# Gate and up as two 64-row tiles side by side in a selective-scan and feed-forward kernel

## The chip, the cores and the metric

The kernel runs on one core of a Trainium2 chip. The metric is the device time of one execution in microseconds (us). A core has five engines with instruction queues of their own: TensorE (PE in the profile; its weight loads are shown as PEld), VectorE (DVE), ScalarE (ACT), GpSimd (POOL) and SyncE (SP), which issues most transfers. PSUM, the memory that TensorE writes, has eight banks here, each 128 partitions by 512 floats.

## The reference, cut to what matters

The input is 2 sequences of 1024 tokens with 512 features, all float32. A selective-scan layer and a feed-forward layer follow, each with a residual and a layer norm:

```python
xn = x * rsqrt(mean(x * x) + 1e-6) * norm_w
xn = xn * sigmoid((xn @ select_proj_w.T + b) * gate)
delta, B, C = split(xn @ x_proj_w.T)              # 128 each
delta = softplus(delta @ dt_proj_w.T + dt_b)      # 512
h = exp(delta * A) * h + (delta * xn) * B         # per token: 512 x 128 states
y = sum over states of h * C
x = layernorm(x + (y + x * D) @ out_proj_w.T)
gate, up = x @ w_gate.T, x @ w_up.T               # 512 -> 2048 each
x = layernorm(x + (silu(gate) * up) @ w_down.T)   # 2048 -> 512
```

The recurrence over h is the long part: 512 x 128 states for each of 2048 tokens. The feed-forward layer is the part that the change rewrites: gate and up both contract over the same 512 features of x (called x1 in the kernel) and give 2048 hidden values each.

## The kernel before, in words

**The loop.** The scan is cut into stretches of 32 tokens (st), each into two half-states h of 8 steps; the main loop (from line 819) has 132 half-states, 1056 steps k. The place of a step in its half-state is r = k % 8. One step does 128 x 32 columns of states. On PE it issues first `state_mm` (line 523, writes bu, four matmuls of 64 rows and 256 columns in fp32r, two row halves b = 0, 1 side by side) and then `decay_mm` of the next step (line 510, writes a, four matmuls of the same shape). ACT copies the carried column of h into bu (line 854) and takes the exponential of a (line 529, two instructions). DVE then runs the scan instruction (line 861) over 1024 columns. POOL makes du, the moving operand of bu, two steps ahead (line 487). bu has two buffers, a has two tiles (one step's), so PE can be ahead of DVE by little more than a step.

**What PE does besides.** After these eight matmuls a step has room for other TensorE work.
- y: the products with C (`y_round`, line 538), eight rounds of 16 matmuls per half-state, always of the half-state before; 128 rows, 32 columns wide, four column strips side by side. ROUNDS says at which places r they stand: rounds 0 to 3 at r = 1, rounds 4 to 7 at r = 5. `y_out` copies the result at r = 0 of a later half-state.
- everything else is a set of Python generators, run by the class Work (line 742). A generator yields "P" when its next piece wants a PSUM bank and PE, "H" between two parts of such a piece, and "E" when other engines are to go first. There is one bank for all of them (`misc`, line 200, pool ps_m with one buffer). The generator that has it is the holder; `give_back` (line 760) takes it back at the start of a step when the holder is at "E". `tensor` (line 774) runs one part. PARTS says how many parts a place r earns as credit (3 at most places, 0 where y stands, 2 at r = 7: 17 a half-state); a step runs at most 4 parts.
- the generators are `pre` (projections for later tokens: ss, sel, xp, b, z, uT), `y_add` (one transpose yT per stretch), `post` (the output projection op and the first layer norm), `ffn` (gate and up, then the down projection d) and `silu` (no PE work).
- `busy` (line 801) is a filler whose result nobody reads: one matmul of 64 rows and 256 columns in fp32 into the second half of y's bank. A step with r > 0 that ran fewer parts than PARTS[r] gets one.

**Gate and up (line 664 on).** A tile of 128 tokens has NF/2 = 8 groups f. x1 is transposed by four PE transposes into x1T, four blocks of 128 features on 128 partitions (line 656), and copied by ACT (line 660). A group is 32 matmuls of 128 rows, 128 columns and 128 moving columns (line 672): for each of two blocks b of 128 hidden values gate and up, each over four blocks k of features. All four results lie in one bank; two matmuls are one part, so a group is 8 parts. ACT copies the bank to gu with one instruction of 512 columns (line 682), then `silu` runs on POOL and ACT.

**Order.** Nothing is reordered after this program: each engine runs its instructions in the order in which the loop emits them (the schedule is manual). When the loop ends, the generators that are left run out with six banks (from line 884); this is called the tail below.

**PSUM.** y has one bank (its first half holds y, the second the fillers), the generators one, bu four, a two: all eight.

Of the kernel before, what the change touches and what calls it, by code (L numbers as in the profile page):

```python
# [9 lines left out]
FP = mybir.dt.float32  # L10
# [6 lines left out]
P = 128  # L17
# [2 lines left out]

ROUNDS = ((), (0, 1, 2, 3), (), (), (), (4, 5, 6, 7), (), ())
PARTS = (3, 0, 3, 3, 3, 0, 3, 2)
RMS_EPS = 1e-6
LN_EPS = 1e-5

# [9 lines left out]
def kernel(  # L37
# [16 lines left out]
    nc = tc.nc  # L54
# [3 lines left out]
    B, L, D = out.shape  # L58
# [474 lines left out]
    def y_round(h, b):  # L533

        st, i = divmod(h, 2)
        at = 28 + 28 * b
        for q in range(NM):
            nc.tensor.matmul(  # L538
                ys[ts(q, 32), 0, :],
                cz[st % 2][:, at : at + 32],  # L540
                hs[i][q // 2][:, ts(q % 2, 64), ts(b, 4)],
                start=(b == 0), stop=(b == 7), skip_group_check=True,
            )

    def y_out(h):

# [7 lines left out]
            return  # L554
        work.add(y_add(st, yc), front=True)

    zs = {}

    def touched(st):

# [16 lines left out]
    def y_add(st, yc):  # L577

        yield "E"
        yield "E"  # L580
        yr = post_pool.tile([P, P], FP, tag="yr", name=f"yr_{st}")
        nc.gpsimd.tensor_tensor(yc, yc, pick.unsqueeze(1).to_broadcast([P, P, 4]), ALU.mult)  # L582
        yield "E"
        nc.gpsimd.tensor_tensor(yc[:, :, 0:2], yc[:, :, 0:2], yc[:, :, 2:4], ALU.add)
        nc.gpsimd.tensor_tensor(yr, yc[:, :, 0], yc[:, :, 1], ALU.add)
        yield "E"
        yield "E"
        yield "P"
        ps = misc(f"yT_{st}", 1)
        nc.tensor.transpose(ps[:, 0:P], yr, ident)  # L590
        yield "E"
        ps = ps[:, 0:P].rearrange("p (m t) -> p m t", t=S)
        for tt, lo, hi in touched(st):
            z = zs[tt][:, :, lo - tt * P : hi - tt * P]
            nc.vector.tensor_tensor(  # L595
                z, z, ps[:, :, lo - token(st) : hi - token(st)], ALU.add
            )
            if hi == (tt + 1) * P:
                work.add(post(tt), front=True)

    def post(tt):

# [30 lines left out]
    def ffn(tt, row):  # L633
# [15 lines left out]
        while finished[-1] < tt:  # L649
            yield "E"  # L650
        fetch(4)
        x1T = ffn_pool.tile([P, NM, P], FP, tag="x1T", name=f"x1T_{tt}")
        yield "P"
        ps = misc(f"x1T_{tt}", 2)
        for m in range(NM):
            nc.tensor.transpose(ps[:, ts(m, P)], row[:, ts(m, P)], ident)  # L656
            if m == 1:
                yield "H"
        yield "E"
        nc.scalar.copy(x1T, ps.rearrange("p (m t) -> p m t", t=P))  # L660
        hid = ffn_pool.tile([P, NF, P], FP, tag="hid", name=f"hid_{tt}")
        ready, at = [], 0

        for f in range(0, NF, 2):
            fetch(at + 4)
            yield "P"
            ps = misc(f"gu_{tt}_{f}", 2 * NM)
            for b in range(2):
                w = pieces[at + b].rearrange("p (a k h) -> p a k h", a=2, k=NM)
                for a in range(2):  # L670
                    for k in range(NM):
                        nc.tensor.matmul(  # L672
                            ps[:, ts(2 * a + b, P)], w[:, a, k, :], x1T[:, k, :],
                            start=(k == 0), stop=(k == NM - 1),
                        )
                        if k % 2:
                            if a and k + 1 == NM and not b:
                                fetch(at + 5)
                            yield "E" if a and b and k + 1 == NM else "H"
            at += 2  # L680
            gu = ffn_pool.tile([P, 2, 2 * P], FP, tag="gu", name=f"gu_{tt}_{f}", bufs=2)
            nc.scalar.copy(gu, ps.rearrange("p (a t) -> p a t", a=2))  # L682
            work.add(silu(gu, hid[:, f : f + 2, :], f"{tt}_{f}", ready), front=True)
        while len(ready) < NF // 2:
            yield "E"
# [21 lines left out]
    def silu(gu, dst, name, ready):  # L707


        yield "E"  # L710
        e = ffn_pool.tile([P, 2 * P], FP, tag="e", name=f"e_{name}", bufs=2)
        g = gu[:, 0, :]
# [12 lines left out]
        ready.append(dst)  # L725
# [16 lines left out]
    class Work:  # L742


        def __init__(self):

            self.gens, self.holder, self.left = [], None, 0

        def add(self, gen, front=False, late=False):
            item = [gen, next(gen), late]  # L750
# [23 lines left out]
        def tensor(self):  # L774

            if self.holder is not None:
                if self.holder[1] != "H":
                    return False
                self.left -= 1
                self.step(self.holder)  # L780
                return True
            for item in sorted(self.gens, key=lambda item: item[2]):
                if item[1] == "P":
# [14 lines left out]
        for _ in gen:  # L798
            pass

    def busy(start=False):

        nc.tensor.matmul(  # L803
            ys[:, 1, :], ident[0:64, :], sel_w[0:64, 0, 0:256],
            start=start, stop=True, skip_group_check=True,
        )

    run(pre(0))
    state_diag(1)
    busy(True)  # L810
# [8 lines left out]
    for k in range(NG):  # L819
# [1 line left out]
        st, i = divmod(h, 2)  # L821
        r = k % 8

        if PARTS[r]:
            work.give_back()
        if r == 0:
            c = lot_of[st]
            for d in range(c + 1, 3 if c == 0 else c + 2):
# [48 lines left out]
        credit -= done  # L877
    y_out(2 * NS - 2)
    for b in range(8):
        y_round(2 * NS - 1, b)  # L880
    y_out(2 * NS - 1)
    ps_a.release()
    ps_bu.release()
    bank_pool[0] = tc.alloc_tile_pool(name="ps_m2", bufs=6, space=PSUM)
    for pool in (half_pool, step_pool, pre_pool):
        pool.release()
# [8 lines left out]
def _laid_out(i):  # L895
# [65 lines left out]
```

## Time and profile before

| what | value |
|---|---|
| median of three runs | 2681.81 us (2676.76 to 2682.79) |
| profiled execution, its own time | 2689.41 us |
| span of the profiled execution | 2687.6 us |
| first scan to the end of the last scan | 57.4 to 2618.4 us |
| busy: PE, DVE, ACT, POOL | 2488.7, 2424.6, 1767.1, 1708.3 us |
| mean granted TensorE clock | 0.953 |

The profile is of one execution. Its busy times are sums over an engine's instructions; matmuls are pipelined, so a PE busy 93% says only that some matmul was nearly always in flight. A record is one instruction as the profiler saw it: a float32 matmul leaves two weight loads and two matmul records (two passes), an fp32r matmul one of each. The granted clock is the share of full speed that TensorE was given; it is 1.0 or 0.5 at any moment.

### The profile page before, as it was taken

The numbers are of one execution on the slowest core, as the hardware profiler recorded it, in microseconds if no ns is written. First come the engines' busy times: TensorE is split into PE (matmuls) and PEld (weight loads), VectorE is DVE, ScalarE is ACT, GpSimd is POOL, SyncE is SP. The second block draws the span as 40 slices with busy tenths as digits, with TensorE's granted clock in tenths as the row PEclk, the third lists the DMA queues.
The fourth block names the chain that finished last, engine by engine and source line by source line (L and its number), as shares of the span: only waits on it lengthen the run. The fifth ranks groups of instructions, "written<-read, shape, count | busy, mean of one in ns | idle before, by whom it ended". The sixth has DMA issues, their size and how long they took to land.

```text
span 2687.6 us, 61618 instructions
## 1 busy us (share of the span) xinstructions
PE 2488.7 (93%) x23742; PEld 1824.6 (68%) x23742; DVE 2424.6 (90%) x1283; ACT 1767.1 (66%) x4248; POOL 1708.3 (64%) x1923
## 2 busy tenths in 40 slices
PE   4888999999999999999999989999999999999998
PEld 3555666767667676776767667676776767676677
DVE  4999989999899999999999999999999999999990
ACT  3666666767677576776767667676667767566663
POOL 3656575766567575676757657577666857565553
PEclk6998899999999999999999989999999999999999
DMA  3122442344434452444423434235433444243335
GB/s 126 26 57 60 146 129 68 109 153 130 112 95 130 135 144 71 129 115 152 146 78 113 125 102 140 77 118 153 135 110 105 139 136 132 59 144 88 114 108 196
DMA packets 329009, 309.49 MB, mean 115 GB/s; under 512 B 184896, under 2 KB 257856, under 8 KB 328592
## 3 DMA queue, kind: packets, MB, share of 16 engines
q1 hardware_dynamic: 326656, 303.16, 38.1%
q8 instruction: 192, 3.15, 0.5%
q0 software_dynamic: 800, 1.97, 0.2%
q14 instruction: 97, 0.79, 0.1%
q10 hardware_dynamic: 1264, 0.43, 0.1%
HBM read 263.46 MB, written 41.94 MB: 114 GB/s over the span
## 4 chain that ended last, share of the span: by engine, by line
PE 37%; DVE 14%; ACT 2%; issue 1%; POOL 0%; POOLq 0%; DVEq 0%; ACTq 0%
DVE h L861 13%; PE gu L672 11%; PE y L538 8%; PE bu L523 6%; PE a L510 4%; PE d L693 3%; PE y L803 1%; PE sel L247 1%; ACT a_sb L529 1%; PE op L611 0%; PE xp L247 0%; ACT bu L854 0%; PE x1T L656 0%; DVE stats_a L731 0%; DVE x L699 0%
## 5 line engine op out<-in xcount | busy, mean ns | idle before, releaser
L861 DVE TENSOR_TENSOR_SCAN h<-a_sb,bu 128x1024 f32<-128x1024 f32 x1056 | 2353.1, 2273 | 168.3 <-ACT bu L854 155.2
L487 POOL TENSOR_TENSOR du<-u_r,hot 128x512 fp32r<-128x512 f32 x1056 | 1112.1, 1058 | 598.6 <-PE bu L523 528.0
L529 ACT ACTIVATE a_sb<-a 128x496 f32<-128x496 f32 x2112 | 1122.9, 585 | 83.0 <-PE a L510 71.7
L523 PE MATMUL bu<-du,b_r 64*128 64x256 f32 x4224 | 623.1, 341 | 89.6 <-DVE h L861 73.7
L854 ACT COPY bu<-h 128x32 f32<-128x32 f32 x1024 | 224.3, 219 | 685.4 <-PE bu L523 609.8
L523 PEld LDWEIGHTS bu<-du,b_r 64*128 64x128 f32 x4224 | 396.5, 190 | 358.7 <-issue 156.1
L538 PE MATMUL y<-h,cz 128*32 128x256 f32 x8448 | 556.6, 407 | 0.1
L672 PE MATMUL gu<-x1T,w 128*128 128x128 f32 x4096 | 542.9, 284 | 9.2 <-DVE zT L595 4.8
L510 PE MATMUL a<-ddt,a_r 64*128 64x256 f32 x4224 | 515.7, 295 | 23.9 <-DVE c_sb L305 9.0
L672 PEld LDWEIGHTS gu<-x1T,w 128*128 128x128 f32 x4096 | 485.2, 193 | 55.1 <-ACT gu L682 10.7
L510 PEld LDWEIGHTS a<-ddt,a_r 64*128 64x128 f32 x4224 | 385.8, 191 | 43.5 <-ACT a_sb L529 21.5
L538 PEld LDWEIGHTS y<-h,cz 128*32 128x32 f32 x8448 | 260.0, 115 | 201.0 <-issue 44.3
L693 PE MATMUL d<-w,hid 128*128 128x256 f32 x1024 | 265.5, 400 | 5.2 <-DVE zT L595 3.7
L693 PEld LDWEIGHTS d<-w,hid 128*128 128x128 f32 x1024 | 185.5, 193 | 46.4 <-DVE zT L595 4.6
L803 PE MATMUL y<-sel_w,ident 64*128 64x256 f32 x572 | 195.8, 423 | 0.0
L713 POOL TENSOR_SCALAR gu<-gu 128x256 f32<-128x256 f32 x128 | 108.1, 845 | 125.7 <-ACT gu L682 125.5
L722 POOL TENSOR_TENSOR hid<-gu,e 128x256 f32<-128x256 f32 x128 | 93.5, 730 | 40.4 <-ACT e L719 38.7
L682 ACT COPY gu<-gu 128x512 f32<-128x512 f32 x128 | 75.1, 587 | 61.8 <-PE gu L672 60.3
L803 PEld LDWEIGHTS y<-sel_w,ident 64*128 64x128 f32 x572 | 88.4, 192 | 34.5 <-issue 21.4
L714 POOL TENSOR_TENSOR gu<-gu 128x256 f32<-128x256 f32 x128 | 93.4, 729 | 10.7
L582 POOL TENSOR_TENSOR yc<-yc,pick 128x512 f32<-128x512 f32 x66 | 68.7, 1041 | 32.8 <-ACT yc L552 32.8
L247 PE MATMUL sel<-xT,sel_w 128*128 128x256 f32 (+1 forms) x288 | 69.5, 381 | 10.0 <-ACT dt L289 6.0
(120 smaller groups left out, 1217.4 us busy)
## 6 DMA issues: line engine op xcount, KB each, us to landing
w<-in_wgu_s_dram SPq DMA_DIRECT2D x256, 512.0 KB, 3.9
w<-in_wd_s_dram SPq DMA_DIRECT2D x128, 512.0 KB, 3.8
u_r<-u_d SPq DMA_DIRECT2D x262, 64.0 KB, 3.1
ddt<-dt_d SPq DMA_DIRECT2D x934, 16.0 KB, 2.2
b_r<-b_d SPq DMA_DIRECT2D x130, 64.0 KB, 3.2
u_d<-uTh SPq DMA_DIRECT2D x15, 512.0 KB, 3.7
u_d<-uT SPq DMA_DIRECT2D x15, 512.0 KB, 4.7
dt_d<-xT SPq DMA_DIRECT2D x56, 128.0 KB, 2.1
```

The source lines that it names most:

```text
L247: nc.tensor.matmul(ps[:, 0:n], w[:, k, ts(m, P)], rhs[:, k, :], start=(k == 0), stop=(k == NM - 1),)
L487: nc.gpsimd.tensor_tensor(dus[k], us[h][:, :, ts(4 * mm + 2 * pair + s, 16)].unsqueeze(3).to_broadcast([P, 2, 16, 16]), hot16.unsqueeze(1) ...
L510: nc.tensor.matmul(ps[:, ts(e, 8), :], a_r[rows, pair, 4 * (2 * i + mm) + x, :], ddts[i][rows, :, 2 * x + mm, :], start=(e == 0), stop=(e ...
L523: nc.tensor.matmul(bu[:, ts(b, 16), ts(j, 16)], prepared[k // 16][rows, j, :], du[rows, j, :, :], start=(j == 0), stop=(j == 1), skip_grou ...
L529: nc.scalar.activation(a_sb[:, k % 3, ts(b, 16), 1:], ps[:, :, 1:], AF.Exp, scale=-1.0)
L538: nc.tensor.matmul(ys[ts(q, 32), 0, :], cz[st % 2][:, at : at + 32], hs[i][q // 2][:, ts(q % 2, 64), ts(b, 4)], start=(b == 0), stop=(b == ...
L672: nc.tensor.matmul(ps[:, ts(2 * a + b, P)], w[:, a, k, :], x1T[:, k, :], start=(k == 0), stop=(k == NM - 1),)
L693: nc.tensor.matmul(ps[:, 0:HD], hid[:, f, :], w[:, f % 4, :], start=(f == 0), stop=(f == NF - 1),)
L713: nc.gpsimd.tensor_scalar_max(g, g, -80.0)
L803: nc.tensor.matmul(ys[:, 1, :], ident[0:64, :], sel_w[0:64, 0, 0:256], start=start, stop=True, skip_group_check=True,)
L854: nc.scalar.copy(bu[:, :, 0], states[:, :, S - 1])
L861: nc.vector.tensor_tensor_scan(states.rearrange("p q t -> p (q t)"), a_sb[:, k % 3, :, :].rearrange("p q t -> p (q t)"), bu.rearrange("p q ...
```

## The change

- The weights of gate and up are laid out anew on the host: in each piece partitions 0 to 63 hold gate, 64 to 127 up, in eight blocks k of 64 features (up's blocks are turned by one).
- x1T gets eight blocks: block j holds features 64j to 64j+63 on the lower partitions and the next 64 on the upper. So each half of the partitions has all 512 features. This takes seven transposes and two small matmuls, in two pieces with a bank, two parts and an ACT copy each.
- A group f is now 64 matmuls of 64 rows: for each b and k one for gate on the lower 64 rows and one for up on the upper 64, in turn. Gate's results go to the generators' bank, up's to the second half of y's bank. Four matmuls (two k) are one part; a group is again 8 parts.
- ACT copies up and then gate, 256 columns each, in place of one copy of 512.
- y and up share a bank, and a `start` flag clears flags of the bank. `begin_y` and `begin_up` therefore keep account of who starts first; a group of gate and up asks for PE with "Q", which is granted while y's rounds are not under way, or once in between when y has started the bank.
- ROUNDS puts y's runs at r = 1 and r = 3; PARTS is 3 at the six other places (18 a half-state). `give_back` runs at every place.
- Fillers: where a place with PARTS ran fewer than two parts and no generator holds the bank, `busy` issues one or two pairs of 64-row matmuls, the lower into the generators' bank and the upper into y's (the lower alone while y's rounds are under way).
- `y_add` waits until the stretch before it is summed; silu's exponential is written over gate; in the tail up takes a bank of its own from the six.

```diff
-ROUNDS = ((), (0, 1, 2, 3), (), (), (), (4, 5, 6, 7), (), ())
-PARTS = (3, 0, 3, 3, 3, 0, 3, 2)
+ROUNDS = ((), (0, 1, 2, 3), (), (4, 5, 6, 7), (), (), (), ())
+PARTS = (3, 0, 3, 0, 3, 3, 3, 3)
...
+        if b == 0:
+            work.begin_y()
+        first = b == 0 and work.y_first
...
-        x1T = ffn_pool.tile([P, NM, P], FP, tag="x1T", name=f"x1T_{tt}")
...
+        x1T = ffn_pool.tile([P, 2 * NM, P], FP, tag="x1T", name=f"x1T_{tt}")
+        for m in range(0, 2 * NM, 4):
+            yield "P"
+            ps = misc(f"x1T_{tt}_{m}", 2)
+            for k in range(4):
+                at = 64 * (m + k)
+                if at + P <= D:
+                    nc.tensor.transpose(ps[:, ts(k, P)], row[:, at : at + P], ident)
+                else:
+                    nc.tensor.matmul(ps[0:64, ts(k, P)], row[:, at:], ident, start=True, stop=True)
+                    nc.tensor.matmul(ps[64:P, ts(k, P)], row[:, 0:64], ident, start=True, stop=True)
+                if k == 1:
+                    yield "H"
+            yield "E"
+            nc.scalar.copy(x1T[:, m : m + 4], ps.rearrange("p (m t) -> p m t", t=P))
...
-            yield "P"
-            ps = misc(f"gu_{tt}_{f}", 2 * NM)
+            yield "Q"
+            lo = misc(f"gu_{tt}_{f}", 2 * NM)
+            hi, first = work.begin_up(f"up_{tt}_{f}")
             for b in range(2):
-                w = pieces[at + b].rearrange("p (a k h) -> p a k h", a=2, k=NM)
-                for a in range(2):
-                    for k in range(NM):
+                w = pieces[at + b].rearrange("p (k h) -> p k h", h=P)
+                for k in range(2 * NM):
+                    for a, ps in enumerate((lo, hi)):
                         nc.tensor.matmul(
-                            ps[:, ts(2 * a + b, P)], w[:, a, k, :], x1T[:, k, :],
-                            start=(k == 0), stop=(k == NM - 1),
+                            ps[:, ts(b, P)], w[ts(a, 64), k, :], x1T[ts(a, 64), k, :],
+                            start=(k == 0 and (a == 0 or first and b == 0)), stop=(k == 2 * NM - 1),
+                            skip_group_check=True,
                         )
...
-            nc.scalar.copy(gu, ps.rearrange("p (a t) -> p a t", a=2))
+            nc.scalar.copy(gu[:, 1, :], hi[:, 0 : 2 * P])
+            nc.scalar.copy(gu[:, 0, :], lo[:, 0 : 2 * P])
...
+        def begin_y(self):
+
+            if self.up_open and not self.up_first:
+                while self.up_open:
+                    self.tensor()
+                    self.give_back()
+            self.y_first = not self.up_open
+            self.y_open, self.up_clear = True, self.y_first
+
+        def up_ready(self):
+            return self.tail or not self.y_open or self.up_clear
+
+        def begin_up(self, name):
+
+            self.up_open, self.up_first = True, self.tail or not self.y_open
+            self.up_clear = False
+            if self.tail:
+                return bank_pool[0].tile([P, 512], FP, tag="m", name=name), True
+            return ys[:, 1, :], self.up_first
...
-    def busy(start=False):
+    def busy(name, count):
 
-        nc.tensor.matmul(
-            ys[:, 1, :], ident[0:64, :], sel_w[0:64, 0, 0:256],
-            start=start, stop=True, skip_group_check=True,
-        )
+        if work.holder is not None:
+            return
+        lo = misc(name, 0)
+        for _ in range(count):
+            for a in range(1 if work.y_open else 2):
+                nc.tensor.matmul(
+                    (lo[:, 0:256], ys[:, 1, :])[a], ident[ts(a, 64), :],
+                    sel_w[ts(a, 64), 0, 0:256], start=(a == 0), stop=True, skip_group_check=True,
+                )
...
-        if r and done < PARTS[r]:
-            busy()
+        if PARTS[r] and done < 2:
+            busy(f"fill_{k}", 2 - done)
...
-    gu = gu.reshape(2, -1, P, d // P, P).transpose(1, 4, 0, 3, 2).reshape(-1, P, 2 * d)
+    gu = gu.reshape(2, -1, P, d // 64, 64).transpose(1, 0, 4, 3, 2)
+    gu = np.stack([gu[:, 0], np.roll(gu[:, 1], -1, axis=2)], axis=1).reshape(-1, P, 2 * d)
```

More of the change, by code (lines that the diff above doesn't have):

```diff
@@ L541, in y_round @@
                 hs[i][q // 2][:, ts(q % 2, 64), ts(b, 4)],
-                start=(b == 0), stop=(b == 7), skip_group_check=True,
+                start=first, stop=(b == 7), skip_group_check=True,
             )
+        if b == 7:
+            work.y_open = False
     def y_out(h):
@@ L555, in y_out @@
         work.add(y_add(st, yc), front=True)
-    zs = {}
+    zs, summed = {}, []
     def touched(st):
@@ L587, in y_add @@
         yield "E"
+        while len(summed) < st:
+            yield "E"
         yield "P"
@@ L599, in y_add @@
                 work.add(post(tt), front=True)
+        summed.append(st)
     def post(tt):
@@ L651, in ffn @@
         fetch(4)
-        x1T = ffn_pool.tile([P, NM, P], FP, tag="x1T", name=f"x1T_{tt}")
-        yield "P"
[L654 to L660, printed above, removed]
+        x1T = ffn_pool.tile([P, 2 * NM, P], FP, tag="x1T", name=f"x1T_{tt}")
[11 more added lines that the diff above has]
+                    yield "H"
+            yield "E"
+            nc.scalar.copy(x1T[:, m : m + 4], ps.rearrange("p (m t) -> p m t", t=P))
         hid = ffn_pool.tile([P, NF, P], FP, tag="hid", name=f"hid_{tt}")
@@ L665, in ffn @@
             fetch(at + 4)
-            yield "P"
-            ps = misc(f"gu_{tt}_{f}", 2 * NM)
+            yield "Q"
+            lo = misc(f"gu_{tt}_{f}", 2 * NM)
+            hi, first = work.begin_up(f"up_{tt}_{f}")
             for b in range(2):
-                w = pieces[at + b].rearrange("p (a k h) -> p a k h", a=2, k=NM)
-                for a in range(2):
-                    for k in range(NM):
+                w = pieces[at + b].rearrange("p (k h) -> p k h", h=P)
+                for k in range(2 * NM):
+                    for a, ps in enumerate((lo, hi)):
                         nc.tensor.matmul(
-                            ps[:, ts(2 * a + b, P)], w[:, a, k, :], x1T[:, k, :],
-                            start=(k == 0), stop=(k == NM - 1),
-                        )
[L676 to L679, printed above, removed]
+                            ps[:, ts(b, P)], w[ts(a, 64), k, :], x1T[ts(a, 64), k, :],
+                            start=(k == 0 and (a == 0 or first and b == 0)), stop=(k == 2 * NM - 1),
+                            skip_group_check=True,
+                        )
+                    if k % 2:
+                        if k + 1 == 2 * NM and not b:
+                            fetch(at + 5)
+                        yield "E" if b and k + 1 == 2 * NM else "H"
             at += 2
+            work.up_open = False
             gu = ffn_pool.tile([P, 2, 2 * P], FP, tag="gu", name=f"gu_{tt}_{f}", bufs=2)
-            nc.scalar.copy(gu, ps.rearrange("p (a t) -> p a t", a=2))
+            nc.scalar.copy(gu[:, 1, :], hi[:, 0 : 2 * P])
+            nc.scalar.copy(gu[:, 0, :], lo[:, 0 : 2 * P])
             work.add(silu(gu, hid[:, f : f + 2, :], f"{tt}_{f}", ready), front=True)
@@ L710, in silu @@
         yield "E"
-        e = ffn_pool.tile([P, 2 * P], FP, tag="e", name=f"e_{name}", bufs=2)
-        g = gu[:, 0, :]
+        g = e = gu[:, 0, :]
         nc.gpsimd.tensor_scalar_max(g, g, -80.0)
@@ L747, in __init__ @@
             self.gens, self.holder, self.left = [], None, 0
+            self.y_open = self.y_first = self.up_open = self.up_clear = self.tail = False
+        def begin_y(self):
[13 more added lines that the diff above has]
+            return ys[:, 1, :], self.up_first
         def add(self, gen, front=False, late=False):
@@ L782, in tensor @@
             for item in sorted(self.gens, key=lambda item: item[2]):
-                if item[1] == "P":
+                if item[1] == "P" or item[1] == "Q" and self.up_ready():
                     self.holder = item
@@ L799, in run @@
             pass
-    def busy(start=False):
-        nc.tensor.matmul(
-            ys[:, 1, :], ident[0:64, :], sel_w[0:64, 0, 0:256],
-            start=start, stop=True, skip_group_check=True,
-        )
+    def busy(name, count):
[8 more added lines that the diff above has]
+                )
     run(pre(0))
     state_diag(1)
-    busy(True)
+    nc.tensor.matmul(ys[:, 1, :], ident, sel_w[:, 0, 0:256], start=True, stop=True)
     bank_pool.pop().release()
@@ L822 @@
         r = k % 8
-        if PARTS[r]:
-            work.give_back()
+        work.give_back()
         if r == 0:
@@ L874 @@
             done += 1
-        if r and done < PARTS[r]:
-            busy()
+        if PARTS[r] and done < 2:
+            busy(f"fill_{k}", 2 - done)
         credit -= done
+    while work.up_open:
+        work.tensor()
+        work.give_back()
     y_out(2 * NS - 2)
@@ L883 @@
     ps_bu.release()
+    work.tail = True
     bank_pool[0] = tc.alloc_tile_pool(name="ps_m2", bufs=6, space=PSUM)
```

## The prediction

> **What bounds the kernel now.** I read the busy rows first: PE 93%, DVE 90%, so two engines share the limit and neither is enough by itself. Then the group rows, for the scan, gate and up, and the filler:
>
> ```profile
> PE 2488.7 (93%) x23742; PEld 1824.6 (68%) x23742; DVE 2424.6 (90%) x1283; ACT 1767.1 (66%) x4248; POOL 1708.3 (64%) x1923
> ...
> L861 DVE TENSOR_TENSOR_SCAN h<-a_sb,bu 128x1024 f32<-128x1024 f32 x1056 | 2353.1, 2273 | 168.3 <-ACT bu L854 155.2
> ...
> L538 PE MATMUL y<-h,cz 128*32 128x256 f32 x8448 | 556.6, 407 | 0.1
> L672 PE MATMUL gu<-x1T,w 128*128 128x128 f32 x4096 | 542.9, 284 | 9.2 <-DVE zT L595 4.8
> ...
> L803 PE MATMUL y<-sel_w,ident 64*128 64x256 f32 x572 | 195.8, 423 | 0.0
> ```
>
> The reader is to see that DVE stood idle 168.3 us before scans, nearly all of it released by ACT's copy into bu, which itself waits for PE's bu. So where DVE idles, PE was late. Next the timeline of PE in a stretch of gate and up:
>
> ```profile
> 1306.04 0.40 PE L510 MATMUL a<-ddt,a_r 64*128 64x256 f32 x4
> 1306.37 2.05 PE L672 MATMUL gu<-x1T,w 128*128 128x128 f32 x16
> 1308.35 0.51 PE L523 MATMUL bu<-du,b_r 64*128 64x256 f32 x4
> 1308.70 0.40 PE L510 MATMUL a<-ddt,a_r 64*128 64x256 f32 x4
> 1309.03 2.05 PE L672 MATMUL gu<-x1T,w 128*128 128x128 f32 x16
> 1311.01 0.51 PE L523 MATMUL bu<-du,b_r 64*128 64x256 f32 x4
> ```
>
> A step with four parts of gate and up takes PE 1311.01 - 1308.35 = 2.66 us. Undisturbed scans start 2.178 us apart (single records; five in a row take 10.97 us with the last one's 2.28). So such a step is 0.48 over DVE's beat. Last, PE's timeline where it has little to do, and the granted clock of one stretch there:
>
> ```profile
> 2325.60 0.79 PE L523 MATMUL bu<-du,b_r 64*128 64x256 f32 x4 [0.29 <-DVE h L861]
> ...
> 2328.93 2.88 PE L538 MATMUL y<-h,cz 128*32 128x256 f32 x32
> 2331.74 0.51 PE L523 MATMUL bu<-du,b_r 64*128 64x256 f32 x4
> ```
> ```profile
> core 0: us, PE busy (x) PEld busy (x) DVE busy (x) ACT busy (x) POOL busy (x), PEclk, DMA share, GB/s
> ...
> 2327.50:2331.50 4.00, 3.72 (x40) 2.19 (x40) 4.00 (x3) 1.92 (x5) 3.29 (x6) 0.57 0.22 25
> ```
>
> The same y run that takes 1.94 us elsewhere takes 2.88 here, at a granted clock of 0.57. I sorted all records by step. From the first scan to the start of the last, 2558.6 us are: 1055 beats of 2.178 = 2297.8; DVE's other work, 65.4; idle time of DVE at full clock, 136.0 (after steps of four parts of gate and up 52.9, of three 10.8, after y 33.6, sel 11.8, d 8.3, the rest 18.6); idle time beside halved clock, 59.4, in some 37 halved stretches, so 1.6 us each. These terms are what the change can move. Before the loop lie 57.4 us, after it 69.0.
>
> **Gate and up.** The change doubles the matmuls (2048 to 4096, as many records again) and halves their rows. Today's records: after a's last matmul the first of gate and up starts 209 ns later, the second 213 ns after that, then one every 111.5, and bu starts 204 ns after the last. bu and a are already pairs of 64 rows: two start within 4 ns, the next pair 224 ns after a switch of shape, then 118 to 120. The new pairs I cost at 118.5, the nearest row; the other end is 111.5, what a pass of 128 rows and as many moving columns takes. A step of four parts was 2.656; now it is 4 pairs of bu and a with 16 of gate and up, all of one shape, 20 x 0.1185 = 2.37; of three parts 16 x 0.1185 = 1.90 (was 2.21), below the beat. So the stream gains nothing; the two switches of shape are what goes.
>
> The Trainium skill's TensorEngine Tiling, Theoretical Speedup, promises gains for a contraction of 64 or less; this one is 512 and filled the rows, so by that page alone nothing is gained and the sum below ends 44 higher. The rows agree on the stream (118.5 against 111.5) and not on the total, because of the switches.
>
> In the program's new order the loop has 156 steps of four parts, 84 of three (before 135 and 97). Deficit 0.48 left 0.398 idle a step, a share of 0.83. So 156 x 0.19 x 0.83 = 25, of which steps of three and two parts, now with 0.28 and more to spare, refill about half: 14. Against it: 46 groups start in the step right after the one before ended, and must wait for both copies. Before, copy 0.59 after the last pass let gate start 0.75 after bu (PEld waited 10.7 us in all for it). Now two copies of 0.38 (the rows of y's copy, 128x256) end 0.92 after, so such a start comes at 0.96 and those steps gain nothing: +6. Gate and up: 63.7 becomes 20, **-44** (bounds: -60 at 111.5 with everything refilled; 0 if the waits eat it).
>
> **The second copy on ACT.** 2 x 0.38 against 0.587: 0.18 x 128 = 23 us. Behind the copies in ACT's queue stand the copy into bu and two exponentials, and the scan waits for those. ACT was busy 66%, so this counts only where PE is late: 287 of 1055 scans waited for that copy, about a third at such places. **+8** (0 to 23). POOL's silu waits 0.18 longer, with idle time beside it.
>
> **Other steps.** With 18 parts a half-state instead of 17, d runs in 73 steps of four (53 before), each 2.60, 0.42 over the beat: +8; sel4 45 against 33 at 0.37 idle each: +4. y keeps its 2.54 (0.36 over) but both runs now lie two steps apart, and PE's lead, at most 1.95 - 0.81 = 1.14 us between bu and scan, has less time to refill: **+6**, from -34 (all its idle gone) to +60 (every y step costs 0.36). Together **+18**. Each half-state has only 18 parts at most, which limits this. x1's five further matmuls and second copy fall into 15 more light steps; covered there by 0.8 us of slack, 15 x 1.3 = 20 if not. Weight pieces keep size and order on SP's queue.
>
> **Fillers and clock.** Clock windows are 3.41 us long. In those after which the clock halved, PE streamed 0 to 0.54 of the time; in those that stayed full, 0.45 to 0.90, with 0.57 at the lowest twentieth. A step with one filler streams 0.47 (four pairs of bu and a) and 0.43 (two passes of 0.213) of its 2.178, a share of 0.41. Two pairs stream 0.47 + 0.87, 0.62. That is on the safe side, and 145 steps have it. But steps with a part of yT, x1T, uT or z now have none: 125 light steps without filler, 10 before. yT alone streams 0.25. Where PE is late they pass in 1.1 us and don't matter; x1's two in a row, and yT among fillers, may drop the clock. I take 24 halved stretches instead of 37: 38 us, **-21** (-59 if all vanish, +140 if each unfilled light step makes one).
>
> The Trainium skill's TensorE: Matmul & The Clock Gate (HAM oscillation) asks only for no idle gap over about 3.4 us. Ahead of the stretch shown above the clock halved at 2323.9 with no gap over 1.1 us between matmuls, so the trace speaks against that. By the page the term would be 0 and the time 21 higher.
>
> **Tail.** d's left-over is 16 records of about 0.22 less: -3.6; 256 pairs at 118.5 for 256 passes at 111.6: +1.8; x1: +1.8. **0.**
>
> **Sum.** -44 + 8 + 18 - 21 = -39: the profiled execution's 2689.4 becomes 2650. The median before lies 7.6 under that execution; taking the difference from 2681.8 gives **2643**.
>
> **Rivals.**
> - *It is as forecast* (2615 to 2672): 0.48.
> - *The fillers do their whole work*: no halved clock, 2643 - 38 = 2605. For: 0.62 is above nearly all windows that dropped. Against: the 125 bare light steps. 0.15.
> - *Pairs run no better in sum*: if a pair took 140 ns, a step of four parts is 0.47 + 2.24 = 2.71, no shorter than 2.656, and -44 becomes 0: 2687, no change. For: twice the instructions, a weight load of 128 columns for each half. Against: bu and a at 118 to 120. That the halves don't run side by side at all (223 a pair, +336 us or more) the records of bu exclude. 0.12.
> - *Slower: bare light steps halve the clock.* Place: yT, x1T, uT, z, which lost their filler. Price 1.6 us each. With 60 halved stretches instead of 24: 2643 + 36 x 1.6 = 2701. It turns to slower from 24 + 24 = 48, when three in eight of them start one. For: 0.25 is below every share of a window that stayed full. Against: a window of 3.41 us also takes in a neighbour, y or gate and up, at 0.85 and more. 0.25 (2687 to 2720).
>
> **Chances and range.** Within 0.2% is what a measurement of this kernel can't tell from no change: 2676 to 2687. Faster 0.48 + 0.15 = 0.63, same 0.12, slower 0.25. The range 2600 to 2705 leaves out about 0.06 below and 0.12 above.
>
> **What the profile after would show.** Steps of four parts with bu 2.4 apart and no gap of 0.2 us between a and gate and up; pairs of gate and up within 5 ns, 112 to 120 apart. DVE's idle time before scans near 130 us (168.3 before), ACT busy near 1800. Halved stretches in the light steps: about 24, none in steps with two pairs of fillers. y still 1.94. It would be wrong if ACT's copies stand in the releasers before gate and up by over 30 us, or if more than 45 stretches are halved.

## The result, and the profile after

| | before | after |
|---|---|---|
| median (runs) | 2682.3 us (2676.8 to 2686.0) | 2765.7 us (4: 2755.9 to 2769.9) |
| ratio to before, 95% interval | | 1.0307 [1.0275, 1.034] |
| span of the profiled execution | 2687.6 us | 2765.2 us |
| from the first scan to the start of the last | 2558.6 us | 2635.0 us |
| idle of DVE in it, at full clock / beside halved clock | 136.0 / 59.4 us | 176.5 / 95.1 us |
| mean granted clock; halved stretches in the loop | 0.953; 40 | 0.963; 34 |

The kernel is slower by 83 us, where 39 less were forecast. (The rows on DVE's idle time and on halved stretches are made as in the prediction, from all records sorted by step; I count 40 stretches before where the prediction said some 37. How a step at the edge of a halved stretch is counted moves some us, up to 9 in one kernel below, from one half of the split to the other; the sum of the two halves is firm.) The page of the changed kernel, the lines that answer to those shown of before:

```profile
PE 2453.3 (89%) x28376; PEld 1855.1 (67%) x28376; DVE 2429.7 (88%) x1283; ACT 1767.5 (64%) x4392; POOL 1712.8 (62%) x1923
...
L903 DVE TENSOR_TENSOR_SCAN h<-a_sb,bu 128x1024 f32<-128x1024 f32 x1056 | 2355.3, 2273 | 239.6 <-ACT bu L896 227.4
...
L687 PE MATMUL gu<-x1T,w 64*128 64x128 f32 x4096 | 558.1, 286 | 44.2 <-DVE zT L602 30.8
L687 PE MATMUL y<-x1T,w 64*128 64x128 f32 x3840 | 515.0, 286 | 60.7 <-ACT yc L557 60.7
```

DVE's scans are as long as before (2273 ns each) and its idle time ahead of them grew from 168.3 to 239.6 us. PE's busy time fell, so PE was not given more to do: it stood. The last two lines say where. Gate's half ("gu") stood 44 us, 31 of them for DVE's addition into zT; up's half ("y", because it is written to y's bank) stood 61 us, all for ACT's copy of y. Before, the one such line had 9.2. The waits of the changed kernel (engine, what and line that waited; what it waited for: us in total, times, longest):

```profile
DVE h L903 <- ACT bu L896: 227.4, 323, 3.8
...
PE y L687 <- ACT yc L557: 60.7, 57, 1.2
...
PE gu L687 <- DVE zT L602: 30.8, 29, 1.3
...
PE y L846 <- ACT yc L557: 24.0, 26, 1.6
...
PE op L619 <- DVE zT L602: 19.3, 16, 1.7
```

Two releasers, then: yc (y's copy) and zT (yT's reader). The timeline at a place r = 0 shows the first:

```profile
949.70 0.37 ACT L699 COPY gu<-y 128x256 f32<-128x256 f32 x1 [0.77 <-PE y L687]
...
949.97 0.38 ACT L700 COPY gu<-gu 128x256 f32<-128x256 f32 x1
...
950.23 0.23 ACT L896 COPY bu<-h 128x32 f32<-128x32 f32 x1
950.38 1.07 ACT L529 ACTIVATE a_sb<-a 128x496 f32<-128x496 f32 x2
...
950.40 0.49 PE L687 MATMUL gu<-x1T,w 64*128 64x128 f32 x2 [0.26 <-ACT gu L700]
...
951.32 0.39 ACT L557 COPY yc<-y 128x256 f32<-128x256 f32 x1
...
951.76 0.37 PE L687 MATMUL y<-x1T,w 64*128 64x128 f32 x1 [0.88 <-ACT yc L557]
```

Up may not write to y's bank before y has been copied out of it, although it writes the other half of it. The copy comes at r = 0, and in ACT's queue it stands behind the two copies of gate and up, the copy into bu and two exponentials: 949.70 to 951.71 us. PE stands from 950.9 on. The copy itself takes 0.39. The second, a step after yT, and the windows around it:

```profile
1004.04 0.33 PE L597 MATMUL yT<-ident,yr 128*128 128x128 f32 x1 [0.34 <-ACT gu L700]
...
1004.89 0.50 PE L523 MATMUL bu<-du,b_r 64*128 64x256 f32 x4 [0.52 <-DVE h L903]
...
1005.42 0.51 PE L510 MATMUL a<-ddt,a_r 64*128 64x256 f32 x4
...
1006.83 0.26 DVE L602 TENSOR_TENSOR zT<-zT,yT 128x124 f32<-128x124 f32 x1
...
1007.15 0.58 PE L687 MATMUL gu<-x1T,w 64*128 64x128 f32 x1 [1.21 <-DVE zT L602]
```
```profile
core 0: us, PE busy (x) PEld busy (x) DVE busy (x) ACT busy (x) POOL busy (x), PEclk, DMA share, GB/s
...
1004.00:1007.20 3.20, 1.39 (x11) 0.85 (x11) 3.20 (x4) 2.58 (x7) 3.12 (x5) 0.86 0.85 256
1007.20:1011.00 3.80, 3.80 (x36) 3.80 (x38) 2.09 (x1) 0.60 (x2) 0.57 (x1) 0.50 0.17 66
```

yT is in the generators' one bank, and the bank is free only when DVE has added it into zT. DVE does that after the scans that stand ahead of it. Until then gate can't start: PE is busy 1.39 of 3.20 us, and after that its clock is 0.50, so the step of gate and up, now late, runs at half speed as well. From one bu to the next PE takes 5.41 us for such a step (median of 17 of the 29 that follow yT). The other 12 keep the full clock through their work and take 4.18, an undisturbed step 2.28. So the wait costs PE 1.9 us by itself, and the halved clock 1.2 more where it comes.

Sorted by step, DVE's idle time was 72 us in the 57 steps of gate and up at r = 0 (12 us in as many steps before), and 58 us in the 29 steps of gate and up and the 15 of op that follow yT. Before, y followed yT in 51 of 65 steps (with a filler between them, which writes to y's bank as y does); neither uses the generators' bank. With y's second run moved from r = 5 to r = 3, yT still comes mostly at r = 4 (37 of 64), and gate and up (29), op (15) and others follow it; y 7 times.

### The profile page after: what moved, and what is told of

Its sections match the earlier page's. It is cut to its first block, busy times and chain, and to the rows that moved or that the text cites. A ratio compares the mean times of both kernels' runs of the same rounds, so it can differ in the third digit from the quotient of the medians.

```text
span 2765.2 us, 70926 instructions
## 1 busy us (share of the span) xinstructions
PE 2453.3 (89%) x28376; PEld 1855.1 (67%) x28376; DVE 2429.7 (88%) x1283; ACT 1767.5 (64%) x4392; POOL 1712.8 (62%) x1923
## 4 chain that ended last, share of the span: by engine, by line
PE 51%; DVE 34%; ACT 9%; issue 4%; DMA 1%; POOL 1%; SPq 0%; POOLq 0%; ACTq 0%; DVEq 0%
DVE h L903 32%; PE y L541 10%; PE gu L687 9%; PE bu L523 7%; PE d L711 6%; PE y L687 5%; PE a L510 5%; ACT a_sb L529 3%; PE sel L247 2%; PE op L619 2%; PE xp L247 1%; PE fill L846 1%; ACT bu L896 1%; ACT gu L700 1%; ACT yc L557 1%
## 5 line engine op out<-in xcount | busy, mean ns | idle before, releaser
L903 DVE TENSOR_TENSOR_SCAN h<-a_sb,bu 128x1024 f32<-128x1024 f32 x1056 | 2355.3, 2273 | 239.6 <-ACT bu L896 227.4
L523 PE MATMUL bu<-du,b_r 64*128 64x256 f32 x4224 | 582.6, 335 | 46.4 <-DVE h L903 35.1
L687 PE MATMUL gu<-x1T,w 64*128 64x128 f32 x4096 | 558.1, 286 | 44.2 <-DVE zT L602 30.8
L687 PE MATMUL y<-x1T,w 64*128 64x128 f32 x3840 | 515.0, 286 | 60.7 <-ACT yc L557 60.7
L687 PEld LDWEIGHTS gu<-x1T,w 64*128 64x128 f32 x4096 | 514.1, 198 | 60.5 <-DVE zT L602 36.8
L687 PEld LDWEIGHTS y<-x1T,w 64*128 64x128 f32 x3840 | 478.6, 198 | 72.1 <-ACT yc L557 72.1
L541 PE MATMUL y<-h,cz 128*32 128x256 f32 x8448 | 517.8, 386 | 1.6 <-DVE h L903 1.0
L846 PE MATMUL fill<-sel_w,ident 64*128 64x256 f32 x580 | 165.8, 400 | 14.4 <-DVE zT L602 4.1
L846 PE MATMUL y<-sel_w,ident 64*128 64x256 f32 x416 | 118.1, 406 | 24.3 <-ACT yc L557 24.0
L739 POOL TENSOR_TENSOR hid<-gu 128x256 f32<-128x256 f32 x128 | 94.0, 734 | 39.3 <-ACT gu L736 30.8
L846 PEld LDWEIGHTS fill<-sel_w,ident 64*128 64x128 f32 x580 | 99.3, 193 | 25.8 <-DVE x L623 6.3
```

What stands on the lines that cost most here:

```text
L523: nc.tensor.matmul(bu[:, ts(b, 16), ts(j, 16)], prepared[k // 16][rows, j, :], du[rows, j, :, :], start=(j == 0), stop=(j == 1), skip_grou ...
L541: nc.tensor.matmul(ys[ts(q, 32), 0, :], cz[st % 2][:, at : at + 32], hs[i][q // 2][:, ts(q % 2, 64), ts(b, 4)], start=first, stop=(b == 7) ...
L687: nc.tensor.matmul(ps[:, ts(b, P)], w[ts(a, 64), k, :], x1T[ts(a, 64), k, :], start=(k == 0 and (a == 0 or first and b == 0)), stop=(k == ...
L846: nc.tensor.matmul((lo[:, 0:256], ys[:, 1, :])[a], ident[ts(a, 64), :], sel_w[ts(a, 64), 0, 0:256], start=(a == 0), stop=True, skip_group_ ...
L903: nc.vector.tensor_tensor_scan(states.rearrange("p q t -> p (q t)"), a_sb[:, k % 3, :, :].rearrange("p q t -> p (q t)"), bu.rearrange("p q ...
```

## The experiments

Theory: **two waits**, up behind y's late copy in the shared bank, and whatever follows yT behind DVE's addition, with the halved clock in its wake. Rivals: one of the two is all of it; or the pairs themselves are no gain; or steps without a filler lower the clock (the prediction's own rival). All times are medians in us. A (1) marks a single execution; executions of one kernel lie up to some 20 us apart (e12: 2676.6 to 2696.3), so a few us between two rows say nothing.

| run | what it is | time (runs) | before beside it | ratio, interval |
|---|---|---|---|---|
| e1 | after, y copied early | 2603.5 (1) | 2682.3 | |
| e2 | after, yT copied by ACT | 2703.4 (1) | 2682.3 | |
| e3 | both | 2613.8 (4) | 2682.3 | 0.9744 [0.9722, 0.9765] |
| e5 | before, new places alone | 2756.0 (1) | 2682.3 | |
| e6 | e1, yT where it was in after | 2696.7 (1) | 2687.1 | |
| e7 | after, yT four places later | 2689.3 (1) | 2687.1 | |
| e8 | before, fillers' rule alone | 2663.2 (1) | 2687.1 | |
| e9 | e1 again | 2598.4 (4) | 2682.8 | 0.9685 [0.9654, 0.9717] |
| e10 | e9, old gate and up, old fillers | 2739.3 (4) | 2682.8 | 1.0214 [1.0175, 1.0252] |
| e11 | e10, new fillers' rule | 2710.5 (5) | 2682.8 | 1.0105 [1.0068, 1.0143] |
| e12 | e11, yT always just ahead of y | 2689.4 (10) | 2684.1 | 1.002 [1.0005, 1.0036] |
| e13 | e9, yT always just ahead of y | 2598.8 (4) | 2684.1 | 0.9686 [0.966, 0.9711] |
| e14 | e13, fillers on one side | 2617.3 (4) | 2683.2 | 0.9765 [0.9736, 0.9794] |
| e15 | before, e11's fillers' rule, yT always just ahead of y | 2650.3 (4) | 2683.2 | 0.9867 [0.9831, 0.9903] |
| e16 | e13, y's places of before, its copy right after them | 2646.5 (4) | 2683.4 | 0.987 [0.9828, 0.9913] |
| e17 | e16, y's copy late | 2708.9 (1) | 2683.4 | |

**e1, e2, e3: take each wait away.** e1 copies y out right after its last round:

```diff
-        if r == 0 and h > 1:
-            y_out(h - 2)
...
+            if r == 3:
+                y_out(h - 1)
```

> The changed kernel with one edit: y's result is copied out of its bank by ACT right behind its last round at r = 3, and no longer at r = 0 of the next half-state. Bank theory: in the changed kernel each matmul of up (and each upper filler) at r = 0 stands behind that copy, which itself stands behind two exponentials; steps with gate and up at r = 0 left DVE idle for about 72 us in all. This run loses nearly all of that: about 2766 - 70 = 2696, and the waits of up for the copy of y fall from 72 us on the weight loads to under 20. Light-step theory (the clock alone): under 15 us of gain, since the light steps stay as they are. Pair theory (64-row pairs are slower than full passes): no gain.

It gained 162, far more than the bank's wait holds. The program's order shows why: with y copied five places earlier all that hangs on the copy comes earlier too, and yT now stands at r = 0 (43 times) and r = 2 (20), so that y follows it 63 of 65 times. Both waits are gone at once; e1 does not tell them apart. e2 leaves y's copy late and frees yT's bank with a copy by ACT, with DVE adding from that copy:

```diff
+        nc.scalar.copy(yr, ps[:, 0:P])
-        ps = ps[:, 0:P].rearrange("p (m t) -> p m t", t=S)
+        ps = yr.rearrange("p (m t) -> p m t", t=S)
```

> The changed kernel with one edit: ACT copies the transposed y out of the generators' bank and VectorE adds from that copy, so the bank is free again without waiting for VectorE's queue of scans. Theory of the bank behind yT: since y no longer follows yT, the next user of the bank (gate and up, op, d) waits for VectorE's addition, TensorE stands still for over a microsecond, and the clock halves behind that; steps right after yT left about 60 us of idle time. This run then gains 45 to 60 us (2706 to 2721), and halved stretches behind yT, 24 of the 33 in the loop, go to under 8. If the missing filler of the light step is the cause and not the wait, the halved stretches stay and the gain is under 15.

It held: 62 less, halved stretches 19 for 34, and of those that begin in the step after a yT 7 for 26. Of the 72 us idle in gate and up at r = 0 some 46 stayed. e3 does both.

> Both edits together. If the two waits are separate causes the gains add: 2766 - 70 - 50 = 2646, below the kernel before (2682) and near what was forecast for the change. If one hides the other, 2690 to 2700. If pairs themselves or the two copies of ACT are the cost, it stays above 2740.

Better than expected, for e1's reason; and 10 to 15 above e1, because the addition became dear (below, at the hardware).

**e5: the places alone, on the kernel before.** Only the first two lines of the diff, ROUNDS and PARTS.

> The kernel before with nothing but the new places and parts (y at r = 1 and 3, three parts at the six other places). Theory of the bank behind yT: yT now is followed by users of the bank instead of y, so 15 to 40 us slower, 2697 to 2722, with new waits of gate and up for the addition of yT. Bank theory: nothing of it is here (no up in y's bank), so it says no change. Light-step theory: no change, as the filler behind yT stays in this kernel.

Of the change's loss nearly all comes with two lines that touch neither gate nor up: +74, more than I had expected. There are 51 halved stretches, and the wait of gate and up on zT, 5.9 us in 5 waits before, is here:

```profile
PEld gu L672 <- DVE zT L595: 32.5, 27, 1.2
...
PE op L611 <- DVE zT L595: 19.4, 16, 1.7
```

**e6 and e7: the two waits apart.** Both put four more waiting points ahead of yT; e6 with y's early copy (which brings yT back to where the changed kernel has it), e7 with the late one.

```diff
-        yield "E"
-        yield "E"
+        for _ in range(6):
+            yield "E"
         while len(summed) < st:
```

> The changed kernel with y copied out right after its last round, as in e1, but with four more waiting points ahead of yT, so that yT stands at the places where it stood in the changed kernel (37 times at place 4) and mostly ahead of gate and up. Theory of two causes: the idle time of TensorE at place 0 (about 72 us in the changed kernel) goes, the loss behind yT (about 60 us beside halved clock) stays: about 2690 to 2700 us. If the wait for the bank was the whole of e1's gain, about 2605 us. If the places of yT were the whole of it, about 2765 us.

> The changed kernel with the copy of y still at place 0, and only four more waiting points ahead of yT: yT then stands at place 0 (38 times) and 2 (21 times), and 59 times y is the next user of the tensor engine after it. Theory of two causes: the stretches at half clock behind yT go, 60 to 90 us, and up still waits for y's bank at place 0: about 2680 to 2700 us. If the bank alone was the cause, about 2765 us; if the places of yT alone were, about 2605 us.

Both came as the theory of two causes had them. Together with after and e9 they make a square:

| | yT ahead of the bank's users | yT ahead of y |
|---|---|---|
| y copied late | 2766 (after) | 2689 (e7) |
| y copied early | 2697 (e6) | 2598 (e9) |

The copy is worth 69 in one column and 91 in the other, yT's place 76 and 98; both together 167, some 22 more than the sum of each alone. e6 and e7 are single executions, so the 22 is rough. The square is not quite clean either: where yT stands at r = 0, gate and up stand there less often, so e7 has 31 waits for y's copy where the changed kernel has 57. Their waits, of e6, e7 and e9 in this order:

```profile
DVE h L901 <- ACT bu L896: 150.7, 237, 2.7
...
PE gu L687 <- DVE zT L602: 26.5, 26, 1.3
...
PE op L619 <- DVE zT L602: 21.9, 16, 1.7
```
```profile
DVE h L903 <- ACT bu L896: 152.7, 220, 5.4
...
PE y L687 <- ACT yc L557: 37.9, 31, 1.3
```
```profile
DVE h L901 <- ACT bu L896: 71.0, 148, 2.6
...
PE y L687 <- ACT yc L557: 10.4, 4, 2.6
```

Each wait stands where its cause was left in and is gone (or nearly) where it was taken away, and DVE's wait ahead of the scans goes from 227 over 151 and 153 to 71. A step after yT in e9, and the window that holds it (columns as above), show how y covers the wait:

```profile
1013.67 0.33 PE L597 MATMUL yT<-ident,yr 128*128 128x128 f32 x1
...
1015.32 1.94 PE L541 MATMUL y<-h,cz 128*32 128x256 f32 x32
...
1016.49 0.32 DVE L602 TENSOR_TENSOR zT<-zT,yT 128x92 f32<-128x92 f32 x2
...
1017.38 0.37 ACT L557 COPY yc<-y 128x256 f32<-128x256 f32 x1 [0.39 <-PE y L541]
...
1017.86 1.99 PE L619 MATMUL op<-out_w,zT 128*128 128x256 f32 x8
```
```profile
1013.50:1017.00 3.50, 2.96 (x47) 1.79 (x43) 3.50 (x5) 3.48 (x8) 2.09 (x2) 1.00 0.00 0
```

y runs its whole 1.94 us while DVE has not yet got to the addition, and the next user of the bank, op, comes after it without a wait. PE is busy 2.96 of 3.50 us and its clock is 1.00. y's copy starts as soon as y is done.

**e8, e10, e11: the fillers' rule.** On the kernel before, and on e9's places of y and early copy with the old gate and up (e10 and e11 have one-sided fillers throughout). This is e8's edit; e11 also asks, as the change does, that no generator holds the bank:

```diff
-        if r and done < PARTS[r]:
-            busy()
+        if PARTS[r] and done < 2:
+            for _ in range(2 - done):
+                busy()
```

> The kernel before with only the rule for fillers made like that of the change (two of them, or one beside one part, in every step without y that has fewer than two parts, and none in steps that had two). What I forecast of it: fewer halved stretches, 24 in place of 37, so some 20 us less, about 2660 us. Rival: the stretches at half clock come from waits in which the engine stands, not from light steps, and fillers do nothing for them: 2675 to 2690 us.

24 less than the one execution of before beside it, with 30 halved stretches for 40: the forecast's size.

> The kernel of e1 again (the change, with y copied out right after its last round), on the same chip as the two kernels beside it. Expected 2595 to 2610 us, as the first time.

> The kernel before with y's places and the early copy of e1, but with its own 128-row gate and up and its own fillers. yT is followed by y in 45 of 65 steps. What the pairs and the fillers are worth is the difference to e1. If the pairs are worth what I forecast (about 44 us) and the fillers some 20, about 2660 us; if the pairs are worth nothing beside the placing of y, about 2605 us.

> The kernel of e10 with the change's rule for fillers (two single ones where there is no part and no generator holds the bank). Against e10 it shows the fillers' worth, against e1 the pairs' worth. By my forecast of the terms, about 2640 us: some 20 below e10, some 35 to 45 above e1. If fillers do nothing, the same as e10 within 8 us.

The fillers gave 29 here. But e10 was 79 above what I expected and e11 70: with y's places moved, the kernel without pairs is slower than before even when y is copied early, and e9 stands 112 below e11. Either the pairs are worth far more than 44, or the order differs: in e11 y follows yT in only 45 of 64 steps.

**e12 and e13: the pairs, with the order held.** Both let yT be given out at r = 0 and 2 alone ("Y" is a mark of its own, taken like "P"; e12 also has the change's rule that `y_add` waits for the stretch before it):

```diff
+                if item[1] == "P" or item[1] == "Y" and self.place in (0, 2):
```

> The kernel of e11 (old 128-row gate and up, the change's fillers, y at places 1 and 3 copied out early) with yT allowed only at places 0 and 2, so that y follows it in 64 of 64 steps as it does in e9. It holds the order of the work equal on both sides of the pairs. If the pairs alone make the 112 us between e11 and e9, about 2705 us. If the order of yT has a share (the halved stretches behind yT in e11 cost some 29 us of idle time by its rows), about 2680 us, and the pairs are worth about 80 us.

> The kernel of e9 with the same rule, yT at places 0 and 2 alone: 65 of 65 steps in place of 63 are followed by y. Expected the same as e9 within its noise, 2590 to 2602 us; it is the partner of the kernel beside it.

Here y follows yT every time (64 of 64, 65 of 65). e12 fell by 21, e13 not at all: the new gate and up, with all that the change brings along for it, and the paired fillers are worth 91. Of e12's loop 134.8 us are idle at full clock and 49.6 beside halved clock; of e13's 84.1 and 13.3.

**e14: gate and up, or the fillers' second half?** e13 with `for a in range(1)` in `busy`.

> The kernel of e13 (pairs of gate and up, y copied early, yT ahead of y) with fillers on the lower 64 rows alone, as in e12, so that against e12 only gate and up differ. e12 to e13 gained 91 us: some 51 us of idle time at full clock and some 36 us beside halved clock. If the 36 us are the fillers' second half, this gives about 2630 us, and gate and up alone are worth about 55 to 60 us. If the steps of gate and up themselves keep the clock, about 2600 us, and all 91 us are theirs.

It came between the two: 18 for the second half of the fillers (25 halved stretches for 11), and **72 for the new gate and up** (e12 to e14). The 72 hold what comes with the pairs: the second copy, x1T's further matmuls, the rule for "Q", silu's exponential written over gate, `give_back` at every place, and fillers in the generators' bank where e12 has them in y's. What these are worth was not tried apart.

**e15 and e16: y's places.** e15 is the kernel before with the fillers' rule of e11 and yT given out at 0 and 4 alone; e16 is e13 with ROUNDS of before, y copied after r = 5, and yT at 0 and 4.

> The kernel before (y at places 1 and 5, old gate and up) with the change's rule for fillers and yT allowed only at places 0 and 4, so that y follows it 65 of 65 times. Against e12 (2689 us), which has the same but y at 1 and 3, it gives the price of y two steps apart with the order of yT held equal. By my forecast of the other steps (18 us, 6 of them y's) about 2671 to 2683 us; by the rows of the kernel with the fillers alone (2663 us, with 14 of 65 yT not ahead of y) about 2645 to 2660 us.

Between e15 and e12 lie **39** us, without pairs and with yT ahead of y on both sides. This is not y's places alone: e12 has 18 parts a half-state for 17, yT at 2 for 4, and y copied early, while e15 has the copy of before, at r = 0. There the fillers that e15's rule puts at r = 0 wait for it, as they do in e8 (27.8 us); e12 has no such wait:

```profile
PE y L807 <- ACT yc L552: 26.5, 19, 1.4
```

So 39 is the price of y's places together with these. From e15 to e12 DVE's idle time at full clock grows by 27 us, 11 of them in the y steps and 11 in gate and up. The gain of e15 on before, 34, has the fillers (24 in e8) and the 14 yT that did not stand ahead of y.

> The kernel of e13 (pairs, paired fillers, y copied right after its last round, yT directly ahead of y) with y's two runs at places 1 and 5 again, so that yT stands at place 4. If the price of y two steps apart (39 us between e15 and e12) adds to the rest, about 2560 us. If the pairs already took that price away (its steps of gate and up no longer need the slack), about 2600 us.

Both expectations missed: with the pairs in place y's old places are 48 **worse** than its new ones. Beside y's places and their copy (and yT at 4 for 2) the order differs in two ways: while y's rounds are open hardly any group of gate and up may begin, so their parts are packed into 204 steps of four (150 in e13) and 36 of three (90), and 101 steps have fillers on one side alone (23); there are 30 halved stretches for 11, and idle time beside them is 33 for 13 us, at full clock 117 for 84. That these two are the cause of the 48 was not tried apart.

> The kernel beside it with the copy of y back at place 0 of the next half-state. Theory: up at place 0 waits for the copy as it did in the changed kernel, at 2 us a step where gate and up stand there: some 40 to 70 us more than beside it. If only yT's order mattered, no difference.

62 above e16 (a single execution): the wait comes back with the late copy at these places of y too. The waits of e17; the line has no counterpart in e16:

```profile
PE y L687 <- ACT yc L557: 58.5, 58, 1.2
```

The best version is the change with y copied right after its last round (e9; e13 is the same within noise): 0.9685 [0.9654, 0.9717] of before.

## Why the prediction was wrong, point by point

From one kernel to the next, as medians: before 2684 to e15, fillers on one side and yT ahead of y, -34; to e12, y two steps apart with 18 parts and the early copy, +39; to e14, gate and up with all that comes along, -72; to e13, fillers' second half, -18; to after, late copy and yT's place, +167 (69 for the copy, 76 for the place, 22 for both at once). That these sum to +82 proves nothing, since each run ends one term and begins the next; and in another order the terms would have other sizes.

- **What bounds the kernel:** right. PE's lateness decides: where PE stood longer, DVE did.
- **Gate and up, -44:** right for what it counted. DVE's idle time at full clock in steps of four and three parts is 58 us in e12 and 15 in e14. The whole difference is 72. A step of four parts takes PE 2.28 us where 2.37 were forecast, for pairs follow each other at the other end of the bounds, 110 to 112 ns:

```profile
952.64 0.27 PE L687 MATMUL y<-x1T,w 64*128 64x128 f32 x1
...
952.65 0.27 PE L687 MATMUL gu<-x1T,w 64*128 64x128 f32 x1
...
952.76 0.27 PE L687 MATMUL y<-x1T,w 64*128 64x128 f32 x1
...
952.76 0.27 PE L687 MATMUL gu<-x1T,w 64*128 64x128 f32 x1
```

  That is 0.10 over the beat, and of the 63.7 us idle in such steps 13 to 15 are left in e9 and e13 (20 forecast). The rest of the 72 lies in other steps (y's idle time at full clock is 36.3 in e12 and 28.7 in e14) and beside halved clock (49.6 and 32.0). That a PE that is less late makes its neighbours less late would explain it, but was not tried. The prediction counted the group alone.
- **What the same step left out, +69: the second step that failed.** It looked for what a group of gate and up waits for and found the two copies of the group before ("46 groups ... must wait for both copies", +6; 12.6 us in 36 waits, so about right). It did not ask who else reads the bank that up was moved to. The reader is y's copy, at r = 0, last in ACT's queue. The prediction's own sign of being wrong, over 30 us of ACT's copies among the releasers before gate and up, came: 60.7 before up, all for this copy.
- **The second copy on ACT, +8:** not measured apart. The two copies overlap: the second starts 0.27 us after the first (949.70 and 949.97 in the timeline above), so both take 0.65 us where one took 0.587, 8 us for 128 groups in place of 23. ACT was busy 1767.5 us (1767.1 before), where 1800 were forecast.
- **Other steps, +18, with "y two steps apart +6": this is the step that failed.** It priced y's move by the slack between two y runs alone. The two lines that make this move, tried alone in e5, cost 74. For the y steps alone the price was fair: DVE's idle time in them at full clock is 34 us before and 38 after. Not seen was who stands behind yT once y has left r = 5 and no longer covers DVE's addition: gate and up, op and others, which then wait. That is worth 76 in the changed kernel (after to e7). With yT's order held, what is left of the move, and of what else differs between e15 and e12, is the 39. The bound of +60 for y would not have held it.
- **Fillers and clock, -21:** about right for the rule by itself (24 in e8, 29 in e11), and 18 more for the paired ones. In the changed kernel it is hidden: 34 halved stretches where 24 were forecast, 26 of which begin in the step after a yT.
- **The rival "bare light steps halve the clock"** named the place, yT, and the side, slower, but for most of the loss not the mechanism. In e2 yT stands where it does in the changed kernel, as bare of fillers; only the bank's wait for DVE is gone, and 7 stretches begin in the step after a yT in place of 26. The rival has a share of what is left: 10 of the 12 halved stretches of e9 begin in a light step without a filler (yT, x1T, uT or z) or in the step after one, and 28 of the 30 of e16 (such steps are 23 in 100 of all), though y follows yT there every time (in e9 63 times of 65). What that costs by itself was not tried. The rival's price, 1.6 us a stretch, was that of a light step; here a full step of gate and up waited 1.9 us and, in 17 of 29 cases, took 1.2 more in a halved stretch.
- **Pairs no better:** refuted by e14 and the records. **Fillers do their whole work:** its 2605 is near the 2600 of e9 and e13, but that is luck: they copy y early, which the change does not, and halved stretches are left in both.

What would have told it in advance was in the profile of before, in its waits:

```profile
PE op L611 <- DVE zT L595: 8.0, 6, 2.1
...
PEld gu L672 <- DVE zT L595: 5.9, 5, 1.2
```

All but one of op's belong to the 14 steps whose yT was not followed by y (the other four have d). Such a step cost DVE 0.7 us in the ten at full clock and 2.2 to 2.8 in the four beside halved clock (two of gate and up, two of op), 1.2 on the average. The order of the changed kernel has 43 more of them: some 53 us by that average, an estimate from before's rows, where yT's place was worth 76.

## What to carry to other kernels

When a change moves a result into a bank that has another user, list who reads that bank, and where the reading instruction stands in its engine's queue: here the wait came from that queue (2 us), not from the read (0.39). When it moves a piece of work in a fixed order, look at what now stands behind its old neighbours: a step that needs nothing from a busy engine may have been the cover for one that does. And a wait of 1.2 to 1.6 us on PE could cost twice in this kernel: 1.9 us of the step by itself, and in 17 of 29 cases 1.2 more at the halved clock that the late step then ran at.

## What the runs showed of the hardware that was not expected

**An addition on DVE that shares its operands' memory with POOL.** In e2 DVE's addition reads yT from SBUF instead of PSUM. Beside POOL's work it takes four times as long, and alone it doesn't:

```profile
939.62 3.09 POOL L487 TENSOR_TENSOR du<-u_r,hot 128x512 fp32r<-128x512 f32 x3
...
941.84 1.00 DVE L603 TENSOR_TENSOR zT<-zT,yr 128x124 f32<-128x124 f32 x1
```
```profile
390.63 0.27 DVE L603 TENSOR_TENSOR zT<-zT,yr 128x124 f32<-128x124 f32 x1
```

Of the 80 additions 42 lay for more than half of their time beside a tensor_tensor of POOL: median 1008 ns, against 262 for the others. With one operand in PSUM, as in the changed kernel, the medians are 257 and 258. The Trainium skill's SBUF — State Buffer (SBUF: two separate sides) says that a VectorE operation with two inputs in SBUF and a GpSimd operation exclude each other for a whole instruction, if the GpSimd operation reads SBUF. These records agree: all 42 began while an operation of POOL ran, and 34 of them ended 120 to 160 ns after one of POOL's ended. In e3 DVE's work other than scans is 97 us where it is 66 in e1, and its idle time is 21 us less, which leaves e3 some 10 us behind.

**Pairs of 64 rows** with 128 moving columns in float32 keep 110 to 112 ns from pair to pair, although each matmul loads weights of its own: the loads (188 ns each in the records) overlap. That is the pace that passes of 128 rows had before (111.5).
